# One over the root by logarithm and exponential, and two products of a convolution moved to GpSimd, in a two-layer convolution and attention kernel

## The chip, the cores and the metric

The kernel runs on one core of one Trainium2 chip. The core has five engines, each with an instruction queue of its own that is worked off in order: TensorE (PE; its weight loads are listed as PEld), VectorE (DVE), ScalarE (ACT), GpSimd (POOL) and SyncE (SP), which here issues most of the DMAs. The metric is the device time of one execution in microseconds (us). The kernel before took 2363.89 us, the median of 3 runs that lie between 2361.51 and 2367.79.

## The reference, cut to what matters

The input is a batch of 8 images of 32 x 32 positions with 256 channels, all in float32. The part that the change touches is the first layer and the attention that follows it:

```
x = x + hybrid(_gn(x), ...)       # _gn: (g - mean) / sqrt(var + 1e-5) over 32 groups of 8 channels
t = x as tokens                   # 8 x 1024 x 256
t = t + attn(_ln_t(t), ...)       # _ln_t: (t - mean) / sqrt(var + 1e-5) over the channels
t = t + ffn(_ln_t(t), ...)        # the same normalisation, then 2 of 8 experts per image
```

`hybrid` joins a 3 x 3 convolution (192 output channels) with an attention of 8 heads of width 8 over the 1024 positions, with relative position terms (64 output channels). `attn` is one head of width 128 over 1024 positions. `ffn` picks two experts for a whole image from the mean of its normalised tokens, and ends with another layer normalisation. Every normalisation needs one over the root of a variance plus a small constant.

## The kernel before

A first phase runs over the images, a second phase runs the experts. Within the first phase an image goes through these stages:

- **Norm** (`norm_steps`, L311 on): PE transposes the image, DVE takes statistics by channel, two small matmuls average them over groups of 8 channels, and `gr` becomes one over the root: an addition of 1e-5 on DVE (L342), a square root on ACT (L343), a reciprocal on DVE (L344). L349 then makes the normalised image `x`. POOL adds the bias of the layer to the image itself (L327).
- **Differences** (`by_fours`): DVE combines columns of `x` into `gdif`, so that the convolution along a row takes six products for four columns (a Winograd form).
- **Inputs** (`input_steps`): projections to keys, queries and values (L412, L433), the relative position terms (`prel`, L484), and their turned form `rwq` (copies L511 on DVE and L513 on ACT).
- **Score, weigh, gather** (`conv_layer_attention`): four units of eight steps. `score` makes the logits to find row maxima (PE L607, DVE reduction L615). Ten steps later `weigh` makes them again with the maximum subtracted (PE L647) and takes the exponential on ACT (L655). `gather` multiplies with the values (PE L664); at the end of a unit its sums are copied to `os` by ACT (L681), and `settle` divides them (DVE L692, L693).
- **Convolution** (`conv_steps`): groups of 12 matmuls (L549) into one PSUM bank `pc`, placed between steps of the score stage. ACT copies a group to `m` (L558, two buffers), and `sums` adds it into the image on POOL: sums and differences `sd` (L524, L525), additions into the image (L521, L528, L532). For the middle one of three pairs, the differences have to be doubled (L527) and the results multiplied by four (L530). Both of these products are on ACT. Two groups of the next image are made early and summed when the own attention begins (`conv.settle`).
- **Second attention** (`attention_layer`): statistics of each token (L813), one over their root through `layer_stats` (L88 to L90), normalised tokens `n` (L823), their transposes copied by ACT to `nT` (L831), projections `pq` (L843) and so on. After it, the statistics `mv2` of the result are turned to one over the root (L956 to L958); POOL then sums the scaled tokens (L966, L968) and sends the image to memory (L973).

The stages of neighbouring images overlap. The norm of the next image runs during the last weigh steps of this one, its inputs during this image's second attention, and its first score steps at that attention's end.

The order of work on PE and POOL is as written in the code during this phase. ACT and DVE are ordered by the framework's scheduler, from the code's order and from estimates of when operands are ready.

ACT evaluates functions from tables. A load of another table appears as ACT_TABLE_LOAD, at the line of the activation that needs it. The code before meets the square root's table early, with activations of one column into `tab` that nothing reads: one at L677 after the last gather of an image, and one back to the exponential at L815.

The routing (from L1115) works on 8 x 8 values between the phases, with a softmax at L1125. In the second phase, `layer_stats` is used too, and stays as it is.

Of the kernel before, what the change touches and what calls it, by code (L numbers as in the profile page):

```python
# [10 lines left out]
FP = mybir.dt.float32  # L11
I32 = mybir.dt.int32
AF = mybir.ActivationFunctionType
ALU = mybir.AluOpType
# [3 lines left out]
P = 128  # L18
B, HH, WW, C = 8, 32, 32, 256
S = HH * WW  # L20
NT = S // P
KC = C // P
NH, DH, DK = 8, 8, 64
HG = 4
NG = NH // HG
# [11 lines left out]
def kernel(  # L37
# [26 lines left out]
    nc = tc.nc  # L64
# [18 lines left out]
    def layer_stats(st, mv, n, eps):  # L83

        for i in range(n):
            nc.vector.bn_aggr(mv[:, i, :], st[:, i : i + 1, :])
        rs = mv[:, 0:n, 1:2]
        nc.vector.tensor_scalar(rs, rs, eps, None, ALU.add)  # L88
        nc.scalar.activation(rs, rs, AF.Sqrt)
        nc.vector.reciprocal(rs, rs)  # L90

    with ExitStack() as ph:
        wp = ph.enter_context(tc.tile_pool(name="wp", bufs=1))
        work = ph.enter_context(tc.tile_pool(name="work", bufs=1))
# [22 lines left out]
        def load_image(b):  # L117
            t = work.tile([P, NT, C], FP, tag="T", name="T", bufs=2)
            eng = nc.gpsimd if b else nc.sync
            eng.dma_start(  # L120
                out=t.rearrange("p (r j) c -> p r j c", j=4), in_=xt[b].rearrange("(r p j) c -> p r j c", p=P, j=4)
            )
            return t

        T = {0: load_image(0)}

        def lg_tile(name):
            return ps_lg.tile([P, 2, 512], FP, tag="lg", name=name)
# [12 lines left out]
        for n, table in (("h", key_rel_h), ("w", key_rel_w)):  # L141
# [21 lines left out]
            out=taps.rearrange("p (n o) -> p n o", o=CO), in_=conv_w.rearrange("a b (k p) o -> p (a b k) o", p=P)  # L163
# [33 lines left out]
            mcols.append(mc)  # L197


        tab = wp.tile([P, 1], FP, tag="tab", name="tab")  # L200
        vall = wp.tile([P, NT, (NH - 1) * (DH + 1) + 32], FP, tag="vall", name="vall")
        nc.gpsimd.memset(vall, 1.0)
        vown = vall[:, :, 0 : NH * (DH + 1)].rearrange("p t (h d) -> p t h d", d=DH + 1)
# [8 lines left out]
        def pt_tile(name):  # L212
            return work.tile([P, 2048], FP, tag="pt", name=name, bufs=4)
# [97 lines left out]
        def norm_steps(b, held):  # L311


            xT = pt_tile("xT").rearrange("p (k s) -> p k s", k=KC)
            st = work.tile([P, KC, 2, 6], FP, tag="gst", name="gst", bufs=2)
            mv = work.tile([P, KC, 2], FP, tag="gmv", name="gmv", bufs=2)
            for kc in range(KC):
                tp = lg_tile("tpx").rearrange("p q (j t) -> p (q j) t", j=4)
                for t in range(NT):
                    nc.tensor.transpose(tp[:, t, :], T[b][:, t, kc * P : (kc + 1) * P], ident)  # L320
                nc.vector.tensor_copy(xT[:, kc, :], tp.rearrange("p t k -> p (t k)"))
                for q in range(2):
                    nc.vector.bn_stats(st[:, kc, q, :], xT[:, kc, q * 512 : (q + 1) * 512])
                yield True
                nc.vector.bn_aggr(mv[:, kc, :], st[:, kc].rearrange("p q s -> p (q s)"))

            nc.gpsimd.tensor_tensor(T[b], T[b], l0b.to_broadcast([P, NT, C]), ALU.add)  # L327
            mean, var = mv[:, :, 0:1], mv[:, :, 1:2]

            pm = st_tile("pm")  # L330
            nc.tensor.matmul(pm[:, 0:KC], lhsT=gavg, rhs=mv[:, :, 0], start=True, stop=True)
            gm = work.tile([P, KC, 1], FP, tag="gm", name="gm", bufs=2)
            nc.vector.tensor_copy(gm[:, :, 0], pm[:, 0:KC])
            dm = work.tile([P, KC, 1], FP, tag="dm", name="dm", bufs=2)
            nc.vector.tensor_tensor(dm, mean, gm, ALU.subtract)
            nc.vector.tensor_tensor(dm, dm, dm, ALU.mult)
            nc.vector.tensor_tensor(dm, dm, var, ALU.add)
            yield True
            pv = st_tile("pv")
            nc.tensor.matmul(pv[:, 0:KC], lhsT=gavg, rhs=dm[:, :, 0], start=True, stop=True)  # L340
            gr = work.tile([P, KC], FP, tag="gr", name="gr", bufs=2)
            nc.vector.tensor_scalar(gr, pv[:, 0:KC], 1e-5, None, ALU.add)  # L342
            nc.scalar.activation(gr, gr, AF.Sqrt)  # L343
            nc.vector.reciprocal(gr, gr)  # L344
            xn = f_tile("x").rearrange("p a e s -> p (a e s)")[:, 0 : KC * S]
            xn = xn.rearrange("p (k a c j x) -> p k a c j x", k=KC, a=2, j=4, x=16)
            for kc in range(KC):
                for a in range(2):
                    nc.vector.tensor_scalar(  # L349
                        xn[:, kc, a],  # L350
                        xT[:, kc, a * 512 : (a + 1) * 512].rearrange("p (j x c) -> p c j x", j=4, x=16),
                        gm[:, kc, :],
                        gr[:, kc : kc + 1],
                        ALU.subtract,
                        ALU.mult,
                    )
            held["xn"] = xn
# [159 lines left out]
        def sums(four, pair, m):  # L517

            add = nc.gpsimd.tensor_tensor
            if pair == 2:  # L520
                add(four[:, 0:4:3], four[:, 0:4:3], m, ALU.add)  # L521
                return
            sd = work.tile([P, 2, CO], FP, tag="sd", name="sd")
            add(sd[:, 0], m[:, 0], m[:, 1], ALU.add)  # L524
            add(sd[:, 1], m[:, 0], m[:, 1], ALU.subtract)  # L525
            if pair:
                nc.scalar.mul(sd[:, 1], sd[:, 1], 2.0)  # L527
            add(four[:, 0:2], four[:, 0:2], sd, ALU.add)  # L528
            if pair:
                nc.scalar.mul(m, sd, 4.0)  # L530
                sd = m
            add(four[:, 2:4], four[:, 2:4], sd, ALU.add)  # L532

        def conv_steps(b, place):
# [6 lines left out]
            for r in range(2):  # L541
                four = T[b][:, 4 * r : 4 * r + 4, 0:CO]
                for pair in range(3):
# [21 lines left out]
        class Unit:  # L565
# [91 lines left out]
            def gather(self, j, parts):  # L657

                if self.po is None:
                    self.po = po_tile("po")  # L660
                cols = slice(parts[0] * P, parts[-1] * P + P)
                for hl in range(HG):
                    h = self.g * HG + hl
                    nc.tensor.matmul(  # L664
                        self.po[32 * hl : 32 * hl + 32, cols],
                        lhsT=vall[:, j, h * (DH + 1) : h * (DH + 1) + 32],
                        rhs=self.pts[j][:, hl, cols],
                        start=j == 0,
                        stop=j == NT - 1 and parts[-1] == 3,
                    )  # L670
                if parts[-1] == 3:
                    pt = self.pts.pop(j)
                    if j == NT - 1:
                        self.close()
                        if self.g == NG - 1 and self.half:

                            nc.scalar.activation(tab, pt[:, 3, 0:1], AF.Sqrt)  # L677

            def close(self):
                self.os = work.tile([P, 512], FP, tag="os", name="os")  # L680
# [41 lines left out]
        def conv_layer_attention(b, units, kq, rh, rwd, rwq, conv, early, ahead, more, done):  # L722
# [75 lines left out]
            for t in range(NT):  # L798
                nc.tensor.matmul(pp[:, t, :], lhsT=aT[:, t * P : (t + 1) * P], rhs=aw, start=True, stop=True)
            nc.vector.tensor_tensor(T[b][:, :, CO:C], pp, T[b][:, :, CO:C], ALU.add)  # L800
            more(0, 4)


        AHEAD = 2

        def attention_layer(b, fill, conv, maxima):

            st = work.tile([P, NT, 6], FP, tag="lst", name="lst")  # L810
            mv = work.tile([P, NT, 2], FP, tag="lmv", name="lmv")
            for t in range(NT):
                nc.vector.bn_stats(st[:, t, :], T[b][:, t, :])  # L813
            layer_stats(st, mv, NT, 1e-5)
            nc.scalar.activation(tab, mv[:, 0, 1:2], AF.Exp)  # L815
            fill(4.5)
            nT = pt_tile("nT").rearrange("p (k s) -> p k s", k=KC)
            for q in range(2):
                tps = [st_tile("tpn").rearrange("p (j t) -> p j t", j=4) for _ in range(KC)]
                for j in range(4):  # L820
                    t = q * 4 + j
                    n = work.tile([P, C], FP, tag="n", name="n", bufs=2)
# [49 lines left out]
            scale = 1.0 / math.sqrt(U)  # L872
# [79 lines left out]


            m = mv2[:, b]
            rs2 = m[:, :, 1:2]
            nc.vector.tensor_scalar(rs2, rs2, 1e-5, None, ALU.add)  # L956
            nc.scalar.activation(rs2, rs2, AF.Sqrt)
            nc.vector.reciprocal(rs2, rs2)  # L958
            mr = work.tile([P, NT], FP, tag="mr", name="mr")
            nc.vector.tensor_tensor(mr, m[:, :, 0], m[:, :, 1], ALU.mult)  # L960
            acc = work.tile([P, C], FP, tag="n", name="acc", bufs=2)
# [125 lines left out]
    work = ctx.enter_context(tc.tile_pool(name="fwork", bufs=2))  # L1087
# [63 lines left out]
    for k in range(TOPK):  # L1151
        m = sm([B, 1], f"m{k}")
# [87 lines left out]
    for b in range(B):  # L1240
# [32 lines left out]
        for q in range(2):  # L1273
# [16 lines left out]
            st = work.tile([P, 4, 6], FP, tag="fst", name="fst")  # L1290
            mv = work.tile([P, 4, 2], FP, tag="fmv", name="fmv")
# [14 lines left out]
            y = work.tile([P, 4, C], FP, tag="yo", name="yo")  # L1306
            for j in range(4):
# [5 lines left out]
                out=ot[b, q * 512 : (q + 1) * 512, :].rearrange("(p j) c -> p j c", j=4),  # L1313
# [52 lines left out]
```

## Time and profile before

One execution was taken by the hardware profiler. It took 2361.41 us, and its span from the first to the last instruction is 2359.6 us.

| what | in the profiled execution |
|---|---|
| execution, span | 2361.41 us, 2359.6 us |
| mean granted TensorE clock | 0.983 |
| exponentials of the weights, L655 on ACT | 944, busy 541.6 us |
| products of `sums` on ACT, L527 and L530 | 16 of 363 ns, 16 of 532 ns |
| POOL additions of `sums`, 384 wide (L528) | 32 of 1008 ns |
| small roots on ACT (L343, L89, L957) | 203 to 211 ns each |
| period of an image in the first phase | 226.7 us (L343 at 195.83, 422.55, 649.24) |
| second phase begins | near 1890 us |

How to read the profile: a line of a timeline gives the start in us from the span's begin, the length of the stretch, the engine, the line of the code, the operation, what it writes and reads, and how many instructions were merged. In brackets stands the idle time of the engine before it, and what ended that. A row of a group gives the count after an x, and behind the bar the busy us, the mean ns of one, and the idle time before them with what ended it. The transfers named by SPq and POOLq are issued by those queues.

### The profile page before, as it was taken

How to read it: one execution, taken by the hardware profiler on the slowest of the kernel's cores; microseconds unless marked ns; L12 is line 12 of the kernel's file. 1: busy time of each engine (PE TensorE's matmuls, PEld its weight loads, DVE VectorE, ACT ScalarE, POOL GpSimd, SP SyncE). 2: the span in 40 equal slices, each digit the busy share in tenths (PEclk: the TensorE clock that was granted, in tenths of full speed). 3: DMA queues.
4: the chain of work that ended last, by engine and by line, in shares of the span. 5: the costliest groups of instructions: out<-in, count | busy, mean ns of one | idle time of the engine just before them, and what ended most of it. 6: DMA issues, size and time to landing. Idle time of an engine off the chain costs nothing. (4 is left out here: it accounts for less than half of the span.)

```text
span 2359.6 us, 41847 instructions
## 1 busy us (share of the span) xinstructions
PE 2269.0 (96%) x17273; PEld 1285.9 (54%) x17273; DVE 1470.0 (62%) x2645; ACT 1028.5 (44%) x1717; POOL 475.4 (20%) x446
## 2 busy tenths in 40 slices
PE   6999999999999999999999999999998699999998
PEld 5535653664367436633763376347533466666665
DVE  7776587658756774777477747764872624444443
ACT  2355336534643564266335633564355323333332
POOL 3201230213021102300230023012301032222221
PEclk7999999999999999999999999999998899999999
DMA  3520252225132503250334034303520222222200
GB/s 107 102 46 26 45 101 39 43 43 103 21 56 40 106 8 60 54 93 3 60 76 72 5 57 96 52 8 54 91 39 2 72 77 72 73 79 83 79 36 27
DMA packets 71469, 135.84 MB, mean 58 GB/s; under 512 B 12000, under 2 KB 24168, under 8 KB 69232
## 3 DMA queue, kind: packets, MB, share of 16 engines
q1 hardware_dynamic: 65488, 115.47, 24.7%
q0 software_dynamic: 3056, 15.73, 2.1%
q8 instruction: 137, 2.24, 0.4%
q10 hardware_dynamic: 2736, 1.97, 0.3%
q14 instruction: 52, 0.43, 0.1%
HBM read 53.43 MB, written 25.17 MB: 33 GB/s over the span
## 5 line engine op out<-in xcount | busy, mean ns | idle before, releaser
L615 DVE TENSOR_REDUCE my<-lg 128x32 f32<-128x1024 f32 x512 | 617.5, 1222 | 173.1 <-PE st L647 125.7
L655 ACT ACTIVATE PT<-st 128x512 f32<-128x512 f32 (+1 forms) x944 | 541.6, 632 | 304.7 <-PE st L647 300.2
L647 PE MATMUL st<-F,km 32*128 32x512 f32 x2048 | 545.3, 641 | 14.1 <-DMA F<-mb 8.9
L607 PE MATMUL lg<-km,F 24*128 24x512 f32 x2048 | 503.6, 636 | 1.9 <-DMA F<-kq 1.8
L664 PE MATMUL po<-PT,vall 128*32 128x256 f32 (+1 forms) x3200 | 315.0, 453 | 2.4 <-ACT PT L655 2.4
L664 PEld LDWEIGHTS po<-PT,vall 128*32 128x32 f32 x3200 | 66.9, 108 | 314.2 <-issue 280.3
L607 PEld LDWEIGHTS lg<-km,F 24*128 24x128 f32 x2048 | 143.7, 183 | 163.6 <-issue 124.3
L549 PE MATMUL pc<-convw,gdif 128*128 128x192 f32 x1152 | 230.1, 343 | 0.7 <-ACT convw L296 0.7
L647 PEld LDWEIGHTS st<-F,km 32*128 32x128 f32 x2048 | 177.5, 183 | 91.5 <-issue 47.7
L1296 PE MATMUL py<-w,hT 128*128 128x256 f32 x1024 | 223.6, 379 | 0.0
L1279 PE MATMUL phd<-n2T,w 128*128 128x512 f32 x512 | 223.4, 594 | 0.0
L549 PEld LDWEIGHTS pc<-convw,gdif 128*128 128x128 f32 x1152 | 187.8, 193 | 55.3 <-issue 31.1
L1296 PEld LDWEIGHTS py<-w,hT 128*128 128x128 f32 x1024 | 194.6, 190 | 33.3 <-issue 7.7
L327 POOL TENSOR_TENSOR T<-T,l0b 128x2048 f32<-128x2048 f32 x8 | 36.4, 4551 | 628.7 <-PE tpx L320 628.7
L1279 PEld LDWEIGHTS phd<-n2T,w 128*128 128x128 f32 x512 | 96.8, 191 | 114.8 <-issue 107.6
L1303 DVE TENSOR_TENSOR r<-py,n 128x256 f32<-128x256 f32 x64 | 27.2, 424 | 212.1 <-PE py L1296 211.9
L828 POOL TENSOR_TENSOR T<-T,n 128x256 f32<-128x256 f32 x64 | 47.3, 747 | 402.2 <-DVE n L823 395.9
L1286 ACT ACTIVATE hT<-phd,b1c 128x512 f32<-128x512 f32 x128 | 86.3, 686 | 96.2 <-PE phd L1279 96.0
L881 PE MATMUL lg<-qkv 128*128 128x512 f32 x256 | 121.1, 595 | 0.0
L890 DVE TENSOR_REDUCE nm<-lg 128x1 f32<-128x1024 f32 x64 | 78.1, 1221 | 67.5 <-PE lg L881 67.5
L912 PE MATMUL po<-pt,qkv 128*128 128x256 f32 x512 | 116.5, 380 | 0.0
L912 PEld LDWEIGHTS po<-pt,qkv 128*128 128x128 f32 x512 | 96.7, 190 | 28.4 <-issue 11.0
(250 smaller groups left out, 2541.3 us busy)
## 6 DMA issues: line engine op xcount, KB each, us to landing
F<-rh SPq DMA_DIRECT2D x256, 128.0 KB
F<-kq SPq DMA_DIRECT2D x256, 64.0 KB
F<-rwd SPq DMA_DIRECT2D x256, 64.0 KB
w<-in_L_ffn_W_dram SPq DMA_DIRECT2D x32, 512.0 KB
rwd<-rw SPq DMA_DIRECT2D x16, 512.0 KB
Td<-T POOLq DMA_DIRECT2D x8, 1024.0 KB, 4.2
T<-Td SPq DMA_DIRECT2D x8, 1024.0 KB
out_dram<-yo SPq DMA_DIRECT2D x16, 512.0 KB
```

The costliest lines, as they stand in the source:

```text
L549: nc.tensor.matmul(pc[:, v, :], lhsT=gflat[:, 2 * pair + v, kc, at : at + P], rhs=convw[:, 2 * pair + v, dy, kc * CO : (kc + 1) * CO], sta ...
L607: nc.tensor.matmul(lg[:, a, :], lhsT=self.F[r : r + 24, a, 0, i * P : (i + 1) * P], rhs=KM[self.g][r : r + 24, a].rearrange("p e k -> p (e ...
L615: nc.vector.tensor_reduce(my[:, :, hl], lg.rearrange("p a (y x) -> p y a x", y=WW), AX.XY, ALU.max)
L647: nc.tensor.matmul(st[:, i, :] if len(heads) > 1 else st, lhsT=KM[self.g][r : r + 32, a, e, :], rhs=self.F[r : r + 32, a, e, :], start=Tru ...
L655: nc.scalar.activation(self.pts[j][:, hs, :], st, AF.Exp)
L664: nc.tensor.matmul(self.po[32 * hl : 32 * hl + 32, cols], lhsT=vall[:, j, h * (DH + 1) : h * (DH + 1) + 32], rhs=self.pts[j][:, hl, cols], ...
L881: nc.tensor.matmul(lg[:, h, :], lhsT=qk[0][:, i * P : (i + 1) * P], rhs=qk[1][:, h * 512 : (h + 1) * 512], start=True, stop=True,)
L890: nc.vector.tensor_reduce(nm, lg, AX.X, ALU.max, negate=True)
L912: nc.tensor.matmul(po[:, 0:IB], lhsT=v1[:, jc, :], rhs=pt[:, jc, :], start=jc == 0, stop=jc == NT - 1)
L1279: nc.tensor.matmul(phd, lhsT=ws[k][0][:, kc, f * P : (f + 1) * P], rhs=n2T[:, kc, q * 512 : (q + 1) * 512], start=kc == 0, stop=kc == KC - 1,)
L1286: nc.scalar.activation(hT[:, k * NF + f, :], phd, AF.Gelu, bias=b1c[:, f, k * B + b : k * B + b + 1])
L1296: nc.tensor.matmul(py, lhsT=hT[:, k * NF + f, j * P : (j + 1) * P], rhs=ws[k][1][:, f, :], start=k == 0 and f == 0, stop=k == TOPK - 1 and ...
```

## The change

One over the root becomes exp(-0.5 ln v) with v the variance plus 1e-5, then one Newton step, in a new function:

```diff
+    def one_over_root(out, var, tiny):
+        v, y = tiny("rv"), tiny("ry")
+        nc.vector.tensor_scalar(v, var, 1e-5, None, ALU.add)
+        nc.scalar.activation(y, v, AF.Ln)
+        nc.scalar.activation(out, y, AF.Exp, scale=-0.5)
+        nc.vector.tensor_tensor(v, v, out, ALU.mult)
+        nc.vector.tensor_tensor(v, v, out, ALU.mult)
+        nc.vector.tensor_scalar(v, v, -0.5, 1.5, ALU.mult, ALU.add)
+        nc.vector.tensor_tensor(out, out, v, ALU.mult)
```

One table set is loaded in front, right behind the load of image 0, and the activations into `tab` are gone:

```diff
         T = {0: load_image(0)}
+        nc.scalar.preload_act_table_set("natural_log_exp_and_others")
...
-        tab = wp.tile([P, 1], FP, tag="tab", name="tab")
...
-                        if self.g == NG - 1 and self.half:
-                            nc.scalar.activation(tab, pt[:, 3, 0:1], AF.Sqrt)
```

The three places of the first phase use the new function:

```diff
             gr = work.tile([P, KC], FP, tag="gr", name="gr", bufs=2)
-            nc.vector.tensor_scalar(gr, pv[:, 0:KC], 1e-5, None, ALU.add)
-            nc.scalar.activation(gr, gr, AF.Sqrt)
-            nc.vector.reciprocal(gr, gr)
+            one_over_root(gr, pv[:, 0:KC], lambda n: work.tile([P, KC], FP, tag=n, name=n))
...
+        def root_of_tiles(var):
+            one_over_root(var, var, lambda n: work.tile([P, NT, 1], FP, tag=f"{n}t", name=n))
...
-            layer_stats(st, mv, NT, 1e-5)
-            nc.scalar.activation(tab, mv[:, 0, 1:2], AF.Exp)
+            for t in range(NT):
+                nc.vector.bn_aggr(mv[:, t, :], st[:, t : t + 1, :])
+            root_of_tiles(mv[:, :, 1:2])
...
-            rs2 = m[:, :, 1:2]
-            nc.vector.tensor_scalar(rs2, rs2, 1e-5, None, ALU.add)
-            nc.scalar.activation(rs2, rs2, AF.Sqrt)
-            nc.vector.reciprocal(rs2, rs2)
+            root_of_tiles(m[:, :, 1:2])
```

The two products of `sums` go from ACT to POOL:

```diff
             if pair:
-                nc.scalar.mul(sd[:, 1], sd[:, 1], 2.0)
+                nc.gpsimd.tensor_scalar(sd[:, 1], sd[:, 1], 2.0, None, ALU.mult)
             add(four[:, 0:2], four[:, 0:2], sd, ALU.add)
             if pair:
-                nc.scalar.mul(m, sd, 4.0)
+                nc.gpsimd.tensor_scalar(m, sd, 4.0, None, ALU.mult)
```

## The prediction

> **What bounds the kernel.** I read the page's busy shares first, then who TensorE (PE) waited for, then the timelines of the places named there.
>
> ```profile
> PE 2269.0 (96%) x17273; PEld 1285.9 (54%) x17273; DVE 1470.0 (62%) x2645; ACT 1028.5 (44%) x1717; POOL 475.4 (20%) x446
> ```
>
> PE has work for all but 90 us of the 2359.6 us span, and ACT and POOL have slack. So work taken off ACT is worth nothing as a sum; it is worth what PE waits for at particular places. (The page's chain of waits breaks off in the last microsecond, so it does not help.) PE's waits, with total us, times, longest:
>
> ```profile
> PE pq L843 <- ACT nT L831: 9.7, 7, 1.4
> ...
> PE st L647 <- ACT PT L655: 5.3, 7, 0.8
> ```
>
> "7 times": once in each image that has a successor. The gaps repeat every 226.7 us, so I read image 0 and multiply by 7. First place, ACT's timeline at the end of the attention (start, us, engine, line):
>
> ```profile
> 193.81 2.00 ACT L655 ACTIVATE PT<-st 128x512 f32<-128x512 f32 x3 [1.26 <-PE st L647]
> 195.83 1.28 ACT L343 ACT_TABLE_LOAD   x1
> 197.12 0.20 ACT L343 ACTIVATE gr<-gr 128x2 f32<-128x2 f32 x1
> 197.34 1.28 ACT L655 ACT_TABLE_LOAD   x1
> 198.64 3.90 ACT L655 ACTIVATE PT<-st 128x512 f32<-128x512 f32 x6
> 202.84 6.26 ACT L655 ACTIVATE PT<-st 128x512 f32<-128x512 f32 x9 [0.30 <-PE st L647]
> 209.12 1.28 ACT L677 ACT_TABLE_LOAD   x1
> ```
>
> Until 195.8 ACT waits for PE (1.26 us before three exponentials). Then the next image's norm takes it from exponentials to the root's table and back, and afterwards ACT has no pause but 0.3 us until 209.1. PE in the same stretch:
>
> ```profile
> 197.41 1.12 PE L647 MATMUL st<-F,km 32*128 32x512 f32 x2
> 199.29 1.14 PE L647 MATMUL st<-F,km 32*128 32x512 f32 x6 [0.75 <-ACT PT L655]
> ...
> 206.95 1.90 PE L664 MATMUL po<-PT,vall 128*32 128x512 f32 x10
> 209.16 1.06 PE L664 MATMUL po<-PT,vall 128*32 128x512 f32 x6 [0.30 <-ACT PT L655]
> ```
>
> The named waits are 0.75 and 0.30 us, but the spacing shows more: a busy PE counts a matmul's latency. Eight such matmuls take 1.07 us, so the six at 199.29 are some 1.8 us late.
>
> Second place, ACT while the image turns to its own attention:
>
> ```profile
> 241.16 0.49 ACT L558 COPY m<-pc 128x384 f32<-128x384 f32 x1
> 244.53 0.36 ACT L527 ACTIVATE sd<-sd 128x192 f32<-128x192 f32 x1 [2.88 <-POOL sd L525]
> 244.80 0.99 ACT L513 COPY rwq<-tpw 128x1024 f32<-128x1024 f32 x1
> 245.69 1.08 ACT L831 COPY nT<-tpn 128x512 f32<-128x512 f32 x2
> ```
>
> The first product waits 2.88 us for a sum on POOL. Queued behind it are the copies L513 and nT (L831), whose inputs PE finished near 242.4, and PE's L843 waits for nT until 246.33 (a gap of 1.37 us).
>
> **The change, part by part.**
>
> *Tables.* Before, the groups of ACT show loads at L655 x15, L343, L677, L815, L957 x8 each, L291 and L1125 x1: 49, at 1283 ns. One remains if exponential and logarithm share it; 48 x 1.283 = 61.6 us of ACT go. (L89 and L1286, x16 each, are in the second phase and stay.) Where that is on the path:
>
> At L343, 7 images. The logarithm takes its place at 195.83, the exponential 0.24 later, and the next exponentials of the weights start when their matmuls are ready: 195.35 + 1.16 (the distance from 192.65 to 193.81 a step earlier) = 196.5, not 198.64. Then PE's own spacing rules, 2.07 us a step (201.68 to 203.75): the five remaining steps start at 195.35, 197.4, 199.5, 201.6, 203.7, and the last exponentials run from 203.7 + 1.16 = 204.9 to 206.9 instead of 209.1. That is 2.2 us; I take 2.0. Late next is PE itself, then DVE: the next image's convolution differences fill it from 200.2 to 212.5, and the reciprocal at L692 comes right behind. It must come earlier between them; if it keeps its place, this gain is only 0.4 (the scale gr comes at about 197.1 instead of 197.5). **-14.0 us.**
>
> [...] The row has the ACTIVATE at 197.12, at once after the load from 195.83: no drain, 2.57 for both. [...]
>
> The loads at L815 (224.5), L957 (296.2) and L655 (324.6) lie in ACT's idle time: nothing. L677's delays os by 0.2 us, hidden behind the pk matmuls but in the last image. L1125 in the routing is on a serial path: **-1.3**, once.
>
> *Logarithm, exponential, Newton step.* Before: one addition, a root, a reciprocal: 0.17 + 0.21 + 0.20 and hops of 0.03, about 0.67. After: an addition, two ACTIVATEs at 0.24 with hop, four small DVE operations at 0.20 (L335 to L337 start 0.20 apart when undisturbed): 1.48. So **+0.8 us on each chain**. The trace has no logarithm; the small activations (203 to 210 ns) are the nearest rows. Covers:
> - gr at 195.6: covered by the steps above. In the setup it is open (PE waits 1.46 for x, L349): +0.8.
> - L813's variances, images 0 to 6: n is ready at 225.2, its transpose runs at 227.2, so 2.0 of cover and 1.2 left. In the last image it is open (PE waits 5.37): +0.8.
> - mv2 (L956): POOL's token sums start at 301.82 and POOL then works until its L521 frees m at 317.14; the copy of the next pc runs 317.26 to 317.74, and PE wants that bank at 318.17. Cover 0.43. The reciprocal already stood behind a 1.22 us reduction, so POOL starts 0.6 late: 0.15 an image, **+1.0**. If one more reduction lands inside the chain, 1.2 more each. In the last image open (PE waits 6.65): +0.8.
>
> The preload now heads ACT's queue, ahead of its DMA issues from 0.73 on. The first that matters, rawh, lands by 2.60; its copy at L227 lasted 3.15 us because POOL's memset ran until 5.67 (the same copy of raww: 0.21). 1.3 us later it still ends near 5.8. The filter taps (landed 14.7) are needed by DVE at 48.9. Nothing.
>
> *The products on POOL.* ACT loses 16 x (0.363 + 0.532) = 14.3 us, and above all its wait. The copy L513 then starts near 242.2, nT ends near 244.3, and PE takes its second half when the first four L843 matmuls are issued, 243.08 + 4 x 0.43 = 244.8 instead of 246.33: 1.5 us, 7 images, **-10.5**.
>
> Their price on POOL:
>
> ```profile
> L1234 POOL TENSOR_SCALAR w<-w,wbc 128x1024 f32<-128x1024 f32 x16 | 46.3, 2904 | 24.5 <-DMA w<-in_L_ffn_W_dram 24.5
> L966 POOL TENSOR_SCALAR part<-T,mv 128x256 f32<-128x256 f32 x49 | 45.1, 921 | 4.1
> ```
>
> Two sizes give 2.58 ns an element and 260 ns fixed: 192 wide 0.76, 384 wide 1.25, together 2.0 us. [...] In the score stage (320 to 326) it moves the load of the next image, queued behind on POOL, by up to 1 us; that image is read some 80 us later.
>
> **Sum:** -14.0 - 10.5 + 1.0 + 0.8 (setup) + (0.8 + 0.8 - 0.2 - 1.3 = 0.1, last image and routing) = -22.6. The profiled execution took 2361.4 (1.8 around the span): 2338.8. The median shown is 2.5 higher: **2341**.
>
> **Rivals.**
> 1. *DVE takes ACT's place at the first stall.* For: DVE is full from 197.5 to 212.5. Against: the differences are needed only from 219.35. Gain 7 x 0.4 instead of 14.0: -11.4, so 2352.
> 2. *POOL's late start becomes PE's wait.* For: the tie of 317.14 and 317.17; DVE works in order and reductions of 1.2 us stand ready. One reduction inside the chain gives back 8.4: 2349; two, with rival 1, 2369. With both first gains it takes 3.2 us of lateness beyond the cover to reach the time before; with rival 1 only 1.6, and from there on the change is slower.
> 3. *The change doesn't do what it says: the table is switched between logarithm and exponential.* Then 24 calls need 48 loads again, all inside chains: the variances lose 2.6 - 1.2 = 1.4 an image, mv2 2.6 + 0.15, the first place gains nothing and loses 0.3; 7 x 4.5 + 6 for the ends of the kernel, less 10.5 + 1.3 that stay: about +26, so 2390. Against: an explicit preload names a set that holds both.
>
> **How the numbers follow.** Forecast (2333 to 2347) 0.53; rival 1 or one reduction alone 0.22 (2349 to 2356); mixtures near no change 0.12; rival 2 in full 0.09; rival 3 0.04. A measurement of this kernel can tell 0.3% (7 us) from no change. Faster 0.73, same 0.13, slower 0.14. Low end: 2.2 and 1.5 saved in full and some microseconds from a reordered DVE and ACT queue, which no row bounds: 2330. High end 2363: rival 1 with one reduction (2361) and a little of the rest.
>
> **What would show it.** One load before the second phase. After gr's exponential the weights' exponentials start within 0.3 us, and PE's six late L647 matmuls close up. No wait of ACT for sd, and PE's wait for nT at L843 gone. An image's period 3 us or so under 226.7. Wrong: exponentials still back to back behind PE, L692 still behind the last difference, POOL's L521 ending later than PE's pc by over 0.5 us, or loads at the logarithm.

## The result, and the profile after

The changed kernel took 2352.64 us, the median of 8 executions between 2340.35 and 2354.64, against 2363.47 for the kernel before in the same comparison: a ratio of 0.994 (0.992 to 0.996). Forecast were 2341 us, and 2330 to 2363. The median alone misleads: three of the eight executions lie at 2340.35 to 2344.06 and five at 2352.34 to 2354.64, with nothing between. With ten later executions of the same kernel, eight of 18 took 2338.9 to 2344.1, nine took 2352.3 to 2356.5, and one 2368.3. So there are two questions: why the lower group is where it is, and what the step of some 10 us or more between the groups is.

The profiled execution (2353.93 us) is one of the upper group. The page's span and busy shares, then ACT's groups of the small activations and the loads, then POOL's groups of the two products (line, engine, operation, names and shapes, count; busy us, mean ns; idle before):

```profile
span 2352.0 us, 41910 instructions
...
PE 2271.4 (97%) x17273; PEld 1295.0 (55%) x17273; DVE 1481.2 (63%) x2717; ACT 955.6 (41%) x1645; POOL 504.5 (21%) x478
```

```profile
L97 ACT ACTIVATE ry<-rv 128x8 f32<-128x8 f32 (+1 forms) x24 | 5.0, 210 | 81.4 <-DVE rv L96 81.4
...
L139 ACT ACT_TABLE_LOAD x1 | 1.3, 1283 | 0.7 <-PEq L1362 0.7
```

```profile
L541 POOL TENSOR_SCALAR m<-sd 128x384 f32<-128x384 f32 x16 | 18.7, 1169 | 1.1
...
L538 POOL TENSOR_SCALAR sd<-sd 128x192 f32<-128x192 f32 x16 | 11.0, 686 | 1.5
```

Of 49 loads in the first phase and the routing one is left, at L139 in front. ACT lost 72.9 us of work. PE is busy for 2.4 us more, though it issues the same 17273 matmuls: it ran slower for a while. The first place, on ACT's timeline of image 0 (start, length, line):

```profile
195.69 2.00 ACT L666 ACTIVATE PT<-st 128x512 f32<-128x512 f32 x3 [1.27 <-PE st L658]
197.57 0.22 ACT L97 ACTIVATE ry<-rv 128x2 f32<-128x2 f32 x1
197.81 0.20 ACT L98 ACTIVATE gr<-ry 128x2 f32<-128x2 f32 x1
198.39 2.00 ACT L666 ACTIVATE PT<-st 128x512 f32<-128x512 f32 x3 [0.37 <-PE st L658]
```

The weights' exponentials follow gr after a wait of 0.37 us for PE; before, a table load stood there. (In image 0, just ahead of the first place, PE's work starts 1.88 us later than in the kernel before: PE's st at 197.23 stands for 195.35. Starts in image 0 are compared after taking that off. So the exponentials start at 196.51, where 196.5 was forecast.) The second place, on ACT's and on PE's timeline:

```profile
243.47 1.01 ACT L524 COPY rwq<-tpw 128x1024 f32<-128x1024 f32 x1 [0.54 <-PE tpw L520]
244.38 1.08 ACT L843 COPY nT<-tpn 128x512 f32<-128x512 f32 x2
```

```profile
243.49 1.04 PE L520 MATMUL tpw<-ident,rw 128*128 128x128 f32 x8
244.36 6.17 PE L855 MATMUL pq<-nT,wqkv 128*128 128x512 f32 x14
```

ACT is now held up only by PE's tpw, and the fourteen matmuls into pq run without the pause of 1.37 us. Both gains are there. But the list of PE's waits (total us, times, longest) has one line that has grown and one that is new. Before:

```profile
PE tpn L827 <- DVE n L823: 7.2, 4, 5.4
```

All four of these are in the last image. After:

```profile
PE tpn L839 <- DVE n L835: 12.4, 11, 6.2
...
PE tpa L798 <- DVE kq L440: 3.5, 7, 0.5
```

The seven added waits at tpn are of 0.62 to 0.64 us. There is one in each image but the last, and the same holds for those at tpa.

An undisturbed image now takes 224.25 us instead of 226.70. Followed along PE through image 0, the lead over the kernel before is 2.13 us after the first place, 1.45 after the new wait at tpa, 0.61 after the new wait at tpn, 2.24 once pq runs, and 2.41 ahead of the next image's first place. In this execution one image, the sixth, took 235.08 us. Its windows of 2 and 10 us (start and end; length; busy us and count of PE, its weight loads, DVE, ACT, POOL; granted clock; DMA share; GB/s):

```profile
1348.00:1350.00 2.00, 1.36 (x22) 0.90 (x11) 1.59 (x3) 0.64 (x1) 0.36 (x1) 1.00 0.29 43
1350.00:1352.00 2.00, 2.00 (x69) 1.87 (x68) 0.81 (x1) 0.42 (x1) 1.77 (x3) 0.82 0.17 31
1352.00:1362.00 10.00, 10.00 (x185) 8.61 (x188) 2.26 (x4) 2.59 (x4) 1.99 (x4) 0.50 0.27 107
...
1374.00:1376.00 2.00, 2.00 (x15) 2.00 (x14) 0.00 (x0) 0.54 (x2) 1.73 (x3) 0.70 0.52 80
```

PE counts as busy all the time, yet from 1351.3 to 1375.2 it is granted half its clock. In a later profile without such an image (the experiment e9 below) the same stretch from 1352 to 1362 holds 335 matmuls at full clock instead of 185. This is most of the step: 235.08 - 224.25 = 10.8 us. (The medians of the two groups are 13 us apart; no profile shows what the rest is. A second profile of the upper group, e12 below, has one such image too, of 234.8 us.) What stands ahead of it on PE's timeline:

```profile
1349.71 0.41 PE L839 MATMUL tpn<-ident,n 128*128 128x128 f32 x2 [0.64 <-DVE n L835]
1350.05 1.25 PE L495 MATMUL prel<-kq,bdw 32*64 32x32 f32 x64
```

It is the new wait at tpn, in a stage where PE spends about half of its time on matmuls of 32x32 (prel, 1.2 us of every 2.2). The kernel before has the same stage without this wait. Why tpn waits is on DVE's timeline of image 0:

```profile
225.82 0.17 DVE L102 TENSOR_TENSOR lmv<-lmv,rv 128x8 f32<-128x8 f32 x1
227.11 1.03 DVE L507 COPY rw<-prel 128x512 f32<-128x512 f32 x1 [1.12 <-PE prel L495]
227.99 0.70 DVE L835 TENSOR_SCALAR n<-T,lmv 128x256 f32<-128x256 f32 x2
```

At 226.0 everything for n is ready and DVE idles for 1.12 us. But the scheduler has queued the copy rw, which waits for PE, ahead of n, and n runs only behind it. Before, n ran ahead of the same copy:

```profile
224.74 0.74 DVE L823 TENSOR_SCALAR n<-T,lmv 128x256 f32<-128x256 f32 x2
226.63 1.05 DVE L496 COPY rw<-prel 128x512 f32<-128x512 f32 x1 [1.15 <-PE prel L484]
```

### The profile page after: what moved, and what is told of

Its sections match the earlier page's. It is cut to its first block, busy times and chain, and to the rows that moved or that the text cites. A ratio compares the mean times of both kernels' runs of the same rounds, so it can differ in the third digit from the quotient of the medians.

```text
span 2352.0 us, 41910 instructions
## 1 busy us (share of the span) xinstructions
PE 2271.4 (97%) x17273; PEld 1295.0 (55%) x17273; DVE 1481.2 (63%) x2717; ACT 955.6 (41%) x1645; POOL 504.5 (21%) x478
## 3 DMA queue, kind: packets, MB, share of 16 engines
q8 instruction: 137, 2.24, 0.4%
## 5 line engine op out<-in xcount | busy, mean ns | idle before, releaser
L658 PE MATMUL st<-F,km 32*128 32x512 f32 x2048 | 536.1, 638 | 8.4 <-DMA F<-mb 8.4
L1288 PE MATMUL phd<-n2T,w 128*128 128x512 f32 x512 | 223.5, 595 | 0.0
```

The costliest lines, as they stand in the source:

```text
L658: nc.tensor.matmul(st[:, i, :] if len(heads) > 1 else st, lhsT=KM[self.g][r : r + 32, a, e, :], rhs=self.F[r : r + 32, a, e, :], start=Tru ...
L1288: nc.tensor.matmul(phd, lhsT=ws[k][0][:, kc, f * P : (f + 1) * P], rhs=n2T[:, kc, q * 512 : (q + 1) * 512], start=kc == 0, stop=kc == KC - 1,)
```

## The experiments

The theory: the change gains at both places, as forecast; the 0.8 us longer chain of L813's variances made the scheduler put n behind the copy rw; that costs 0.8 us in every image, and in some images the half clock. Rivals: the products on POOL cause the gap or the clock's fall (POOL late, more traffic); or ACT's shorter work does. Each kernel was compared with the kernel before on the same chip (2363.71 us for e1, e2, e3, e6; 2363.81 for e4, e5, e8, e9; 2363.51 for e10 to e12, one execution each). The us are medians; the ratio is taken over the executions and lies near the ratio of the means, so it is not that of the medians where the executions fall into groups (e6, e9).

| kernel | us (all executions) | ratio to before | undisturbed image |
|---|---|---|---|
| e1, tables alone | 2360.31 (2351.2 to 2373.4) | 0.999 (0.997 to 1.0005) | 225.9 |
| e2, POOL alone | 2351.70 (2349.5 to 2355.9) | 0.994 (0.993 to 0.996) | 225.0 |
| e3, change with early n | 2338.30 (2335.2 to 2339.4) | 0.988 (0.987 to 0.990) | 223.5 |
| e6, before with late n | 2396.11 (2367.8 to 2405.7) | 1.011 (1.007 to 1.014) | 227.5 |
| e9, the change again | 2343.31 (2338.9 to 2368.3) | 0.994 (0.991 to 0.996) | 224.3 |
| e4, no Newton step | 2340.48 (2336.7 to 2347.3) | 0.991 (0.990 to 0.992) | 223.2 |
| e8, tables with early n | 2349.83 (2345.0 to 2350.6) | 0.994 (0.993 to 0.995) | 225.1 |
| e5, both orders | 2333.40 (2328.6 to 2333.6) | 0.987 (0.985 to 0.988) | 222.7 |
| e10, e6 once more | 2386.78 | | 227.5 |
| e11, longer gap | 2428.12 | | 228.2 |
| e12, the change once more | 2352.31 | | 224.3 |

**The two halves of the change.** In e1 the products stay on ACT:

```diff
-                nc.gpsimd.tensor_scalar(sd[:, 1], sd[:, 1], 2.0, None, ALU.mult)
+                nc.scalar.mul(sd[:, 1], sd[:, 1], 2.0)
...
-                nc.gpsimd.tensor_scalar(m, sd, 4.0, None, ALU.mult)
+                nc.scalar.mul(m, sd, 4.0)
```

> The one table and the Newton step as in the change, the two products of the sums back on ACT. Sum of places: the first stall of PE goes (2.2 us an image), of which DVE's order at the reciprocal takes back 0.7 and the late normalised tokens 0.8; PE's wait for nT at the projections stays at 1.4 us. Period of an image about 226.1 us instead of 226.7, fast executions near 2358 to 2360. Theory of the gap (PE's clock halves after the new gap ahead of the transposes of n, in a stage of small matmuls): the gap is still there, so some of the executions lie 8 to 12 us above the others and show a lower granted clock. Rival (the slow executions come from the chip and hit any kernel): as often here as in the kernel before of the same call.

e2 is the reverse edit, made to the kernel before.

> The kernel before with the two products of the sums on POOL, tables and roots as before. PE's wait for nT goes (1.4 to 1.6 us an image), all else stays: period about 225.1 us, time about 2352. Theory of the gap: no gap ahead of the transposes of n, so no group of executions 10 us above the rest. Rival (POOL's longer work or the denser PE brings the slow executions): some executions 8 us or more above the rest.

PE's waits in e1:

```profile
PE tpn L839 <- DVE n L835: 12.4, 11, 6.2
PE pq L855 <- ACT nT L843: 8.4, 6, 1.4
```

With POOL untouched the wait at tpn is the same, to the tenth, and the half clock is there too (one image of 235.1 us in the profile, and executions that differ by up to 22 us). e2 has neither: no wait at tpn in the images that have a successor, no half clock of 24 us in an image, five executions within 6.4 us, and 12.0 us less than before. (Its profile has two shorter half clocks in the images, of 6.8 and 3.4 us, behind waits of 1.24 us for a DMA and of 0.75 us at the first place.) So the gap and the long half clock come from the normalisation, not from POOL. As it stands, the table part is worth 3 us, with an interval that takes in nothing at all.

**The order of n.** e3 is the change with the first two n issued ahead of the filling work, and the copy rw held behind them in DVE's queue:

```diff
+            first = [normed(t) for t in range(2)]
+            behind[:] = [made[-1]]
             fill(4.5)
+            behind.clear()
...
-                            nc.vector.tensor_copy(dst, src)
+                            with tc.issue_after(behind[0]) if behind else ExitStack():
+                                nc.vector.tensor_copy(dst, src)
```

> The change, with DVE made to issue the first two normalised tokens ahead of the copy of rw; nothing else differs. The gap of 0.63 us ahead of the transposes of n goes: period 224.25 - 0.8 = 223.4 us, time about 2334. Theory of the gap: the executions near 2353 disappear, all within 4 us of each other. Rival (slow executions from elsewhere): still two groups 10 us apart, the lower near 2334.

DVE's timeline of e3 at the same place:

```profile
225.45 0.17 DVE L102 TENSOR_TENSOR lmv<-lmv,rv 128x8 f32<-128x8 f32 x1
225.65 0.74 DVE L833 TENSOR_SCALAR n<-T,lmv 128x256 f32<-128x256 f32 x2
226.73 1.06 DVE L508 COPY rw<-prel 128x512 f32<-128x512 f32 x1 [0.34 <-PE prel L495]
```

n fits into the pause, and the copy still starts when PE delivers. The image falls to 223.5 us, the profile has no half clock in these images, and all four executions lie within 4.3 us. The whole chain of logarithm, exponential and Newton step is kept here, so its length is not what cost the time.

e6 makes the same gap in the kernel before, by holding n behind the copy and nothing else:

```diff
-                            nc.vector.tensor_copy(dst, src)
+                            copied = nc.vector.tensor_copy(dst, src).ins
+                            if which == 0 and half == 0:
+                                copies.append(copied)
...
+                    late = copies[-1:] if t == 0 else []
+                    with tc.issue_after(late[0]) if late else ExitStack():
...
```

> The kernel before, with nothing but DVE's order changed: the first normalised tokens stand behind the copy of rw, which makes the gap of the changed kernel ahead of the transposes of n. Period about 227.3 to 227.6 us, fast executions about 2368. Theory of the gap: some executions another 8 to 12 us higher at a lower granted clock, as in the changed kernel. Rival: no such group, as in the kernel before.

The windows of its third image:

```profile
682.00:686.00 4.00, 3.38 (x131) 2.78 (x123) 2.37 (x4) 1.37 (x3) 1.53 (x2) 1.00 0.27 41
686.00:688.00 2.00, 2.00 (x15) 1.57 (x18) 0.06 (x2) 0.47 (x1) 0.72 (x1) 0.53 0.00 0
688.00:698.00 10.00, 10.00 (x206) 8.97 (x203) 2.72 (x5) 2.10 (x4) 2.18 (x3) 0.50 0.27 108
...
710.00:712.00 2.00, 2.00 (x14) 1.52 (x13) 0.71 (x1) 2.00 (x4) 1.00 (x1) 1.00 0.51 66
```

A gap of 0.62 us, and half the clock from 686.1 to 710.0, in three of seven images of this profile (236.7 to 238.2 us each). The old normalisation and the old products do it as soon as n is late: the order alone is enough. And in e3, where n is early and all else is the change, neither the gap nor such a half clock appeared.

e8 joins e1 and the early n.

> One table and the Newton step, the products on ACT, and the first normalised tokens ahead of the copy of rw. Theory: this is the tables' share without the gap. Period 225.9 - 0.85 = 225.05 us, time 2350 to 2352 with executions within some 4 us. With the products on POOL alone also at 2351.7, the two halves each give 12 us and add up to the 25 of both. Rival (the tables' part gains little in itself): 2358 or more.

The tables then give 14.0 us, POOL alone 12.0 (e2), both with the early n 25.4 (e3): the halves add up to within a microsecond, and they did not need each other. The wait for nT is still there in e8 (9.7 us, 7 times), which is POOL's share.

e4 shortens the chain by taking its last four operations out:

```diff
-        nc.vector.tensor_tensor(v, v, out, ALU.mult)
-        nc.vector.tensor_tensor(v, v, out, ALU.mult)
-        nc.vector.tensor_scalar(v, v, -0.5, 1.5, ALU.mult, ALU.add)
-        nc.vector.tensor_tensor(out, out, v, ALU.mult)
```

> The change with the Newton step left out: one over the root is the exponential's value as it is, four small DVE operations fewer on each of the three chains. Theory of the gap: with the chain 0.8 us shorter the scheduler puts the normalised tokens ahead of the copy of rw again, the gap and the half clock go; period 223.4 us, open chains 2.4 us less (setup and twice in the last image), so 2335 to 2336 and no group 10 us above. Rival (the loss comes from logarithm and exponential or from POOL): still 10 us groups.

The scheduler now puts n ahead of the copy by itself; there is no wait at tpn in the images that have a successor, and an image takes 223.2 us. So it was the longer chain that turned the order round. The wait at tpa is gone here too, so this run does not separate the two; e3 does. The median came out some 5 us over what was expected, and the executions spread over 10.6 us, which the theory did not foresee. The profile (2336.71 us) has one half clock of 10 us in another place, at the beginning of a weigh stage, 1.5 us behind a PE wait of only 0.27 us; what brought it is open. The four higher executions have a lower mean clock (0.977 to 0.980 against 0.983 of the two lowest), but no profile shows where it fell.

**The other new wait.** At tpa PE waits for `at`, which DVE makes from rc right behind kq (the list names kq). On DVE's timeline of the change, rc needs pa, which PE has done at 212.3, and is issued at 213.70, behind three more operations of the differences, of which this shows the last:

```profile
213.23 0.55 DVE L409 TENSOR_TENSOR gdif<-gdif,x 128x224 f32<-128x224 f32 x1
213.70 0.25 DVE L700 RECIPROCAL rc<-pa 128x16 f32<-128x16 f32 x1
```

e5 is e3 with those three behind the copy aT:

```diff
+                        rest = by_fours(held["xn"])
+                        for _ in range(17):
+                            next(rest)
+                        with tc.issue_after(turned[0]):
+                            for _ in rest:
+                                pass
```

> The change with both of DVE's orders mended: the first normalised tokens ahead of the copy of rw, and the last step of the convolution's differences behind the copy of aT, so that the reciprocal of the last unit comes 1.4 us sooner. PE's gap of 0.5 us ahead of tpa goes and the step before it closes up: 0.7 us an image against the version with the tokens' order alone. Period about 222.7, time about 2333. If DVE only shifts the same work to where the next item waits for it, no difference: 2338.

DVE's timeline in e5:

```profile
212.24 0.26 DVE L701 RECIPROCAL rc<-pa 128x16 f32<-128x16 f32 x1
...
214.41 0.68 DVE L803 COPY aT<-tpa 64x512 f32<-64x512 f32 x1 [0.86 <-PE tpa L800]
215.02 0.28 DVE L407 TENSOR_SCALAR gdif<-gdif 128x256 f32<-128x256 f32 x1
```

rc runs ahead of them, the seven waits at tpa for kq are gone from the list, and an image takes 0.7 us less than in e3. Nothing is lost by the three operations from 215.0 on. This is the best version: 1.3% under the kernel before.

**Which images fall to the half clock.** e9 is the change itself, on another chip.

> The changed kernel once more, beside the others. Theory of the gap: its executions spread over some 2340 to 2356 or more, each image whose gap halves the clock adding 10.8 us to a floor near 2340. Rival (the spread was chance of one chip or hour): all near one value.

It shows the two groups anew; its profile is of the lower one, with seven gaps at tpn and no half clock. So the gap doesn't always bring it. (The execution of 2368.26 us was not profiled; whether two images fell in it isn't known.) The trace records every change of the granted clock. Those of the first profile of the change, up to 1400 us (start, length, clock):

```
  30.34      6.83  1.0
  37.16     20.48  0.5
  57.64      6.83  1.0
  64.47      6.83  0.5
  71.30   1280.00  1.0
1351.29     23.89  0.5
1375.19    419.84  1.0
```

All lengths are multiples of 3.413 us, and so they are in every profile of this study (but for the last record, which the end of the trace cuts off), each with an offset of its own. That raised the question whether it matters where between two points of this grid the gap ends. Three more kernels asked this: e10 is e6 unchanged, e11 adds a copy on DVE between rw and n, e12 is the change.

```diff
+                        if late:
+                            nc.vector.tensor_copy(n, T[b][:, t, :])
```

> The kernel before with its normalised tokens once more queued behind the copy rw, looked at anew. In every execution so far all changes of the granted clock lie on a grid of 3.413 us, with an offset of its own for each execution. Of 28 gaps of 0.62 to 0.64 us at tpn in four profiles, the five followed by the half clock ended 1.70 to 1.83 us after a grid point; the others ended elsewhere (nearest 1.62 and 1.92). [...] With one image in the band the time is 2390 to 2405; with none 2366 to 2370. Theory B (chance, or the images alternate by themselves): half clocks also at other offsets, or none at offsets in the band.

> As the run before, with one more copy of a token tile (128x256, some 0.4 us) on VectorE between the copy rw and the first normalised tokens; nothing else depends on it. [...] Theory B (what matters is that a gap exists, not its length or place): as many images as with 0.62, up to three, at any offset; the time 3 us above the run before.

> The change itself, once more. Theory A: an image's gap at tpn is followed by the half clock exactly if it ends 1.62 to 1.92 us after a grid point of 3.413 us; with images 224.27 us apart the offsets of neighbouring images differ by 2.38 us, so none or one of the seven falls, seldom two. Time 2339 to 2344 with none, 2352 to 2357 with one. Theory B: half clocks at other offsets, or gaps in the band without one.

The offsets (us from a point of the grid to the gap's end) in the three:

```
e10  2.60  1.43  1.73*  2.83  1.66  0.47  2.70*
e11  3.31* 2.97* 2.68*  2.27* 2.04* 0.23  3.11*     (* half clock follows)
e12  1.40  0.38  2.75*  2.10  1.14  0.21  2.52
```

The band from 1.62 to 1.92 was wrong as an exact rule: two of the three new falls in e10 and e12 are at 2.70 and 2.75, and 1.66 did not fall. Nor did images alternate in e10, and its time with two falls was below the 2390 expected. What held is the grid of 3.413 us, and that in these profiles the falls came at some places between its points and not at others. Over six profiles with 42 gaps of 0.62 to 0.64 us, the eight that tripped ended at 1.70 to 1.83 (six) or 2.70 to 2.75 (two), and no other gap ended in these two bands. With 1.15 us (PE's wait in e11, where the author's estimate was 1.0) six of seven tripped, and the time of 2428 us went past the author's estimate of 2415 at most; by theory B it would have been three images at most, and 3 us above e10 instead of 41. In all fourteen the half clock begins at the first grid point behind the gap's end. The second band was found after the fact and wasn't tried on new executions.

## Why the prediction was right, and where not

- **First place.** Forecast 2.2 us, taken 2.0; measured 2.13. "Late next is PE, then DVE" named what followed: DVE kept rc behind the last differences. The prediction said that it must come earlier or the gain be only 0.4; it kept its place, and 0.7 of the 2.13 was lost, not 1.8. Two things made the rest. The differences begin 0.6 us earlier (x at 198.84, less the 1.9, against 197.56), and rc 0.8; and the copy aT comes 1.53 us after rc, where it came 2.17 after it before.
- **A table's price.** By the row, two loads took 2.57 us, with the ACTIVATE 0.01 to 0.02 us behind each. What came back at this place is 2.13, so the row was a fair measure of it.
- **Second place.** Forecast 1.5 us, measured 1.63; e2 alone gave 12.0 in all against the forecast 10.5.
- **POOL.** The products took 0.69 and 1.17 us, 1.86 together, for the 2.0 estimated from the rows of L1234 and L966. POOL's bias addition started at 249.94, less the 1.88 at 248.06, against 248.22 before, and nobody waited for it. Rival 2 did not happen, but it was near: in image 0 the copy m ended at 317.73 and PE's pc began at 317.81 without a wait, so 0.08 us was left of the cover of 0.43. The 1.0 us that the sum set down for the late POOL was not paid.
- **Chain of 0.8 us.** Measured 0.8 (1.47 against 0.63 at L813). In the setup PE's wait for x grew from 1.46 to 2.29, in the last image the waits grew from 5.37 to 6.18 and from 6.65 to 7.48, and the wait in the routing fell from 2.81 to 1.54: forecast were 0.8 for each of the three, and 1.3.
- **The step that failed** is the cover of L813's variances: "n is ready at 225.2, its transpose runs at 227.2, so 2.0 of cover and 1.2 left". n's operands were ready in time (226.0, with the image's later start). But the step asked only when they are ready and when the result is needed, not what DVE would have queued in between. The copy rw waits for PE until 227.1, and n stood behind it: 0.84 us lost in each image instead of none. And in the upper group, ten of the 18 executions, an image at half clock, 10.8 us, as the two of them that were profiled show.
- **The sum.** In an undisturbed image the change gives 2.45 us instead of the 3.35 forecast; with n in place 3.2 (e3). The lower group, 2338.9 to 2344.1, is where the forecast put the kernel, partly by luck: seven images lost 0.9 each against it, and the profile e9, without a half clock in these images, has a span 18.3 us shorter than before, where 22.6 were forecast. (One span can't measure the missing 4 closely: the same kernel reaches image 0's tpn at 228.27 in e9 and at 224.96 in e12.) The median of eight is 11.6 us over the forecast because five of them are in the upper group, through a half clock that no step of it considered; e9's nine executions have a median of 2343.31. That 2352.64 lies inside the range is luck: the range reached up there for rival 1, which did not come to pass.

## What to carry to other kernels

When a chain grows by less than its cover, look at the queue and not only at the operands: a scheduler that orders by estimates may move an instruction behind one that waits for another engine, and the cure may be to fix the order of two instructions by hand (e3, e5). A table switch or a product on the wrong engine is worth what the next engine waits for behind it (here 2.13 us of PE's time for two loads of 2.57, and 1.63 for two products that took ACT 0.90), and each gain taken exposes the queue order of the engine that is next. When executions of one kernel fall into two groups, compare the period of each stage and the granted clock of its windows first.

## What the runs showed of the hardware

A gap of 0.64 us on PE cost 10.8 us in the sixth image of the change (235.08 against 224.25). In a stage with many matmuls of 32x32, eight of 42 gaps of 0.62 to 0.64 us were followed by a granted clock of 0.50 for 24 us (seven grid steps each) while PE was shown as busy, and the full clock came back 2.5 to 4.2 us after the last of these matmuls. In e11, with 1.15 us, it lasted 17 to 27 us, and one of the six ended while the stage still ran.

The length of a gap alone did not decide. In each of the seven images of the change that have a successor, PE also waits 0.88 to 1.00 us for a DMA ahead of st, among larger matmuls, and no half clock followed. The old wait at the first place, 0.75 us, was followed by a half clock of one step, 3.4 us, in six of 35 cases (in the profiles of the kernel before, e2, e6, e10 and e11). In the kernel before that was at 880.5 us, and its image took 1.5 us longer. The kernels with one table have no gap there.

All changes of the granted clock in these profiles lie on a grid of 3.413 us. Ahead of the eight falls, the stretch between two grid points that held the gap had only 0.6 us without a matmul. PE's idle time in it doesn't tell the cases apart: worked out from the traces, it is 0.62 to 0.64 us for the gaps that ended at 1.43 to 1.66 and brought no half clock, as for those at 1.70 to 1.83 that did.

Whether gaps outside the two bands can bring it, and what part the matmuls of 32x32 have in it, stays open.
